# Key lists in three parts: attention over 64 queries where only one half of a query tile needs the keys

## The chip, the core and the metric

The kernel runs on one NeuronCore of a Trainium2 chip. The metric is the device time of one execution in microseconds. The kernel before takes 2263.21 us (median of three executions, 2261.73 to 2263.39). The profile shown below is of one execution with a span of 2257.2 us.

## What is computed

One layer of a graph transformer over 4096 nodes with 512 features, in float32. The adjacency matrix holds only zeros and ones and is sparse: node i and node j are joined with a probability that falls with both indices, so early nodes have many neighbours and late ones few.

```python
def gnn(node_matrix, adjacency, Wks, Wqs, Wvs, Wo):        # 8 heads of 64
    adj = maximum(adjacency, eye)
    q, k, v = node_matrix @ (Wqs, Wks, Wvs)                # per head
    scores = q @ k.T * 64 ** -0.5 + 0.01 * eye - 1e16 * (1 - adj)
    return einsum('hqm,hmk,hko->qo', softmax(scores), v, Wo)

x = x + gnn(layernorm(x), adj, ...)
x = x + moe_ffn(layernorm(x))       # 8 experts, each token goes to its best 2
```

A masked score has weight zero in the softmax. So for a query only its neighbours and itself have to be looked at.

## The kernel before

The 4096 queries are cut into 32 tiles of 128. For each query tile the kernel makes a list of the keys that at least one of its 128 queries is joined to, gathers those keys' rows 128 at a time, and runs attention on the gathered tiles alone. `LISTED` holds how many list tiles each query tile gets (363 in all); one more tile per query tile is the diagonal one (c = -1), so there are 395 items of attention.

**Stage one** projects x to k, v and q, and builds the lists beside it. Per query tile, VectorE reduces the adjacency to a flag for each key, counts flags, and GpSimd compares slot numbers with the running count (`begun`). TensorE then turns the comparison into the rows of the list with one matmul for each list tile, and VectorE computes the key numbers. `pack` already gathers two fifths of the mask tiles while GpSimd is there, and stores them packed, so that SyncE can fetch them later with a plain transfer.

```python
def neighbours(i):                      # one flag per key: is it joined to any of the 128 queries
    nc.vector.tensor_reduce(flags[g][:, j, :], adj_in.pop(i), axis=AX.X, op=ALU.max)

def begun(i):
    n = listed[i] * P
    nc.gpsimd.tensor_scalar(
        started[i], slots[:, :n], base[g][:, j : j + 1], None, op0=ALU.is_ge)

def list_rows(i, k):
    ...
    for t in range(m):
        nc.tensor.matmul(pr[:, t, :], started[i][:, ts(t0 + t, P)], row_x[g][:, j, :], ...)

def pack():
    i, c = ready.pop(0)
    m = work.tile([P, P], F32, tag="mask", bufs=6)
    gather(m, adjT_rows, mask_of, i, c)
    nc.sync.dma_start(out=packed_d[packed[i, c]], in_=m)
...
        if u < 8 * NTB - 4:             # at the end of each of 60 steps of stage one
            for _ in range(min(3, len(ready))):
                pack()
```

**Attention** runs over the 395 items in order, software-pipelined. Gathers run nine items ahead into ten buffers. In one round of the loop TensorE turns the keys of item n+3, computes the scores of item n+2 and multiplies the values of item n; between them stand pieces of work on query tiles that are done (sums, output projection, gate).

```python
def fetch(n):
    gather(kv[n], kv_d, key_of, i, c)                     # 128 rows of 4 KB, by GpSimd
    if (i, c) in packed:
        nc.sync.dma_start(out=mask[n], in_=packed_d[packed[i, c]])
    else:
        gather(mask[n], adjT_rows, mask_of, i, c)         # 128 rows of 512 B, by GpSimd

def turn(n):            # 8 transposes of 64 x 128
    nc.tensor.transpose(pk[:, r, ts(p, KD)], kv[n][half, ts(p, P)], ident[half, half])
    ...                 # then ScalarE copies PSUM to kT[n]

def scores(n):          # for each of 8 heads: keys are the weights, queries the moving side
    nc.tensor.matmul(s[r][:, p, :], k[rows, p, :], q_in[i][rows, p, :], start=True, stop=True)
    ...
    nc.scalar.activation(e[:, r * NP : (r + 1) * NP], s[r], AF.Exp)

def masked(n):
    nc.vector.tensor_mul(e, e, m.unsqueeze(1).to_broadcast([P, 2 * NP, P]))

def values(n):          # for each of 8 heads: values are the weights, e the moving side
    nc.tensor.matmul(po[i][r * KD : (r + 1) * KD, p, :], v[:, ts(h, KD)], e[:, r * NP + p, :], ...)
    ...
    nc.vector.tensor_add(acc[i], acc[i], e)
```

The profile counts two LDWEIGHTS and two MATMULs for each float32 matmul, and one of each for a transpose. The heads come in pairs that lie in different rows (scores, turn) or columns (values) of the array.

**Stage three** runs the expert layers on the routed tokens. If a list was too short for its keys, a general path recomputes all; with these inputs it does not run.

Of the kernel before, what the change touches and what calls it, by code (L numbers as in the profile page):

```python
# [12 lines left out]
I32 = mybir.dt.int32  # L13
AF = mybir.ActivationFunctionType
# [13 lines left out]
    10, 10, 9, 9, 9, 9, 9, 9, 9, 8, 8, 8, 8, 8, 8, 8,  # L28
]
# [3 lines left out]
def kernel(  # L33
# [50 lines left out]
    listed = [min(n, NT) for n in LISTED]  # L84
    at = [sum(listed[:i]) for i in range(NT + 1)]
# [8 lines left out]
    adjT_rows = adjT.rearrange("i k q -> (i k) q")  # L94

# [15 lines left out]
    longer = const.tile([P, NT], F32, name="longer")  # L111
# [78 lines left out]
    packed_d = dram.tile([NT * max(listed), P, P], F32, name="packed_d")  # L190
    waiting = []
# [11 lines left out]

    def fetch(n):

        i, c = items[n]
        kv[n] = kvp.tile([P, KV], F32, tag="kv", name=f"kv_{i}_{c}")
        mask[n] = kvp.tile([P, P], F32, tag="mask", name=f"mask_{i}_{c}")
        if c < 0:
            nc.sync.dma_start(out=kv[n], in_=kv_d[ts(i, P), :])  # L210
            nc.sync.dma_start(out=mask[n], in_=adjT[i, ts(i, P), :])
            return
        gather(kv[n], kv_d, key_of, i, c)
        if (i, c) in packed:
            nc.sync.dma_start(out=mask[n], in_=packed_d[packed[i, c]])
        else:
            gather(mask[n], adjT_rows, mask_of, i, c)

        if waiting and n % 3 == 0:
            waiting.pop(0)[1]()  # L220
# [9 lines left out]
    with tc.tile_pool(name="wqkv", bufs=1) as wp, tc.tile_pool(name="p1", bufs=3) as work, tc.tile_pool(  # L230
# [18 lines left out]
        for n, src, queue in (("k", Wks, nc.scalar), ("v", Wvs, nc.scalar), ("q", Wqs, nc.sync)):  # L249
            for c in range(DC):  # L250
# [14 lines left out]
        )  # L265

# [10 lines left out]
        slots = lp.tile([P, max(listed) * P], F32, bufs=1, name="slots")  # L277
        nc.gpsimd.iota(slots, pattern=[[1, max(listed) * P]], base=0, channel_multiplier=0,
                       allow_small_or_imprecise_dtypes=True)
# [3 lines left out]
        room = lp.tile([P, NT], F32, bufs=1, name="room")  # L283
        for i in range(NT):
            nc.gpsimd.memset(room[:, i : i + 1], float(listed[i] * P))
        again_c = lp.tile([P, G, C], F32, bufs=1, name="again_c")
        zero = lp.tile([1, KV], F32, bufs=1, name="zero")

        def list_constants():
            nc.vector.tensor_sub(step, ident, step)  # L290
            nc.vector.tensor_mul(other, other, part)
            nc.vector.tensor_scalar(other, other, -1.0, 1.0, op0=ALU.mult, op1=ALU.add)
            nc.vector.memset(again_c, 1.0)
            nc.vector.memset(again_c[:, :, 0:1], 0.0)
            nc.vector.memset(zero, 0.0)
            nc.sync.dma_start(out=kv_d[N : N + 1, :], in_=zero)
# [7 lines left out]
        def neighbours(i):  # L304

            g, j = divmod(i, G)
            if j == 0:
                flags[g] = lp.tile([P, G, C], F32, tag="flags", name=f"flags_{g}")
            nc.vector.tensor_reduce(flags[g][:, j, :], adj_in.pop(i), axis=AX.X, op=ALU.max)  # L309

        def count_1(g):

            f = flags.pop(g)
            nc.vector.tensor_mul(
                f, f, other[:, ts(g, G)].unsqueeze(2).to_broadcast([P, G, C])
            )
            upto = lp.tile([P, G, C], F32, tag="upto", name=f"upto_{g}")
            nc.vector.tensor_tensor_scan(
                upto.rearrange("p j c -> p (j c)"), again_c.rearrange("p j c -> p (j c)"),
                f.rearrange("p j c -> p (j c)"), initial=0.0, op0=ALU.mult, op1=ALU.add,  # L320
            )
            x_g = lp.tile([P, G, NX], BF16, tag="x", name=f"x_{g}")
            nc.vector.tensor_copy(x_g[:, :, :C], upto)
            row_x[g] = x_g

        def count_2(g):
            x_g = row_x[g]
            pb = ps_a.tile([P, 2, G], F32, tag="a", name=f"pb_{g}")
            nc.tensor.matmul(pb[:, 0], below, x_g[:, :, C - 1], start=True, stop=True)
            nc.tensor.matmul(pb[:, 1], ones, x_g[:, :, C - 1], start=True, stop=True)  # L330
            base[g] = pb

        def count_3(g):
            x_g, pb = row_x[g], base[g]
            b = lp.tile([P, G], F32, tag="base", name=f"base_{g}")
            nc.vector.tensor_copy(b, pb[:, 0])
            nc.vector.tensor_tensor(longer[:, ts(g, G)], pb[:, 1], room[:, ts(g, G)], op=ALU.is_gt)  # L337

            most = lp.tile([P, G, NT], F32, tag="most", name=f"most_{g}")
            nc.vector.tensor_tensor(  # L340
                most, b.unsqueeze(2).to_broadcast([P, G, NT]),
                full.unsqueeze(1).to_broadcast([P, G, NT]), op=ALU.is_ge,
            )
            hi = lp.tile([P, G], F32, tag="hi", name=f"hi_{g}")
            nc.vector.tensor_reduce(hi, most, axis=AX.X, op=ALU.add)
            lo = lp.tile([P, G], F32, tag="lo", name=f"lo_{g}")
            nc.vector.scalar_tensor_tensor(lo, hi, -float(P), b, op0=ALU.mult, op1=ALU.add)
            nc.vector.tensor_copy(x_g[:, :, C], hi)
            nc.vector.tensor_scalar_add(x_g[:, :, C + 1], lo, float(P))
            nc.vector.tensor_copy(x_g[:, :, C + 2], number.to_broadcast([P, G]))  # L350
            base[g] = b

        def steps(g):

            pd = ps_a.tile([P, G, NX], F32, tag="a", name=f"pd_{g}")
            nc.tensor.matmul(pd, step, row_x[g], start=True, stop=True)
            x_g = lp.tile([P, G, NX], BF16, tag="dx", name=f"dx_{g}")
            nc.scalar.copy(x_g, pd)
            row_x[g] = x_g

        def begun(i):

            g, j = divmod(i, G)
            n = listed[i] * P
            started[i] = lp.tile([P, n], BF16, tag="started", name=f"started_{i}")
            nc.gpsimd.tensor_scalar(  # L366
                started[i], slots[:, :n], base[g][:, j : j + 1], None, op0=ALU.is_ge
            )
# [4 lines left out]
        def list_rows(i, k):  # L373

            g, j = divmod(i, G)
            t0, m = chunks(i)[k]
            pr = ps_l.tile([P, CHUNK, NX], F32, tag="l", name=f"pr_{i}_{t0}")
            for t in range(m):
                nc.tensor.matmul(
                    pr[:, t, :], started[i][:, ts(t0 + t, P)], row_x[g][:, j, :],  # L380
                    start=True, stop=True,
                )
            rows_of[i, k] = pr

        def list_keys(i, k):
# [20 lines left out]
            nc.vector.tensor_scalar_add(mask_of[:, to], key, float(i * (N + 1)))  # L406
# [99 lines left out]
        def pack():  # L506
            i, c = ready.pop(0)
            m = work.tile([P, P], F32, tag="mask", bufs=6, name=f"pm_{i}_{c}")
            gather(m, adjT_rows, mask_of, i, c)
            packed[i, c] = len(packed)  # L510
            nc.sync.dma_start(out=packed_d[packed[i, c]], in_=m)
# [222 lines left out]
    with tc.tile_pool(name="p2a", bufs=2) as two, tc.tile_pool(  # L734
# [56 lines left out]

        def scores(n):

            i, c = items[n]
            s = [ps_s.tile([P, NP, P], F32, tag="s", name=f"s{r}_{i}_{c}") for r in range(2)]
            k = kT.pop(n)
            for p in range(NP):
                for r in range(2):
                    rows = slice(r * KD, (r + 1) * KD)
                    nc.tensor.matmul(  # L800
                        s[r][:, p, :], k[rows, p, :], q_in[i][rows, p, :],
                        start=True, stop=True,
                    )
            if c < 0:
                e = two.tile([P, 2 * NP, P], F32, tag="acc", name=f"acc_{i}")
                acc[i] = e
            else:
                e = work.tile([P, 2 * NP, P], F32, tag="e", name=f"e_{i}_{c}")
            for r in range(2):
                nc.scalar.activation(e[:, r * NP : (r + 1) * NP], s[r], AF.Exp)  # L810
            es[n] = e

        def masked(n):
            e, m = es[n], mask.pop(n)
            if items[n][1] < 0:
                nc.vector.tensor_max(m, m, eye_d)
            nc.vector.tensor_mul(e, e, m.unsqueeze(1).to_broadcast([P, 2 * NP, P]))  # L817

        def values(n):
# [4 lines left out]
            v = kv.pop(n)[:, H * KD :]  # L824
            for p in range(NP):
                for r in range(2):
# [3 lines left out]
                        po[i][r * KD : (r + 1) * KD, p, :], v[:, ts(h, KD)], e[:, r * NP + p, :],  # L830
# [3 lines left out]
            if c >= 0:  # L834
                nc.vector.tensor_add(acc[i], acc[i], e)  # L835
# [188 lines left out]
        bad = small.tile([P, NT, 3], F32, name="bad")  # L1024
        nc.vector.tensor_single_scalar(bad[:, :, 0], fine[:, :, 0], HIGH, op=ALU.is_lt)
        nc.vector.tensor_single_scalar(bad[:, :, 1], fine[:, :, 1], 1.0 / LOW, op=ALU.is_lt)
        nc.vector.tensor_single_scalar(bad[:, :, 2], longer, 0.5, op=ALU.is_lt)
# [264 lines left out]
```

## Time and profile before

| stage of the trace | us from the span's start | length, us | TensorE busy, us | VectorE busy, us | GpSimd busy, us |
|---|---|---|---|---|---|
| projections and lists (after the start) | 60 to 440 | 380 | 324.8 | 290.6 | 254.5 |
| seam | 440 to 468 | 28 | 20.7 | 5.4 | 13.2 |
| attention | 468 to 1645 | 1177 | 1149.3 | 1040.7 | 860.4 |
| seam | 1645 to 1700 | 55 | 19.4 | 18.2 | 7.8 |
| experts | 1700 to 2257 | 557 | 546.0 | 166.9 | 110.6 |

Busy times are of the instructions themselves; about 0.3 us after each gather in which GpSimd can't start the next is not in them. In the profile, L800 is the scores' matmul, L829 that of the values, L784 the turning of keys; L810 is the exponential, L787 ScalarE's copy of the turned keys; L817 and L835 are VectorE's mask product and sum; L199 is any gather, L366 the comparison of `begun`, L590 the last small matmul of the gate. PE is TensorE, PEld its weight loads, DVE VectorE, ACT ScalarE, POOL GpSimd.

### The profile page before, as it was taken

Reading aid. Unit: us, or ns where it says so; the run is one execution under the profiler, and the core shown is the slowest. Engines: PE = TensorE matmul, PEld = TensorE weight load, DVE = VectorE, ACT = ScalarE, POOL = GpSimd, SP = SyncE. Lnnn points to the kernel's source line nnn. Section 1 sums busy time; section 2 is a strip of 40 time slices with the busy share of each in tenths; the row PEclk is TensorE's granted clock in tenths of the full one; section 3 lists DMA queues with packets and bytes.
Section 4 is the critical chain, followed back from the end, with each engine's and each line's share of the span. In section 5 each row is a group of like instructions: output and inputs, shape, how many; then the busy total and the mean of one; then the engine's idle time right before and its main releaser. Section 6 shows DMA issues by size and latency. Waiting matters only on the chain. (4 is left out here: it accounts for less than half of the span.)

```text
span 2257.2 us, 51565 instructions
## 1 busy us (share of the span) xinstructions
PE 2104.6 (93%) x20304; PEld 1404.5 (62%) x20304; DVE 1550.2 (69%) x2300; ACT 966.7 (43%) x1834; POOL 1252.9 (56%) x943
## 2 busy tenths in 40 slices
PE   7788887989999999999999999999839999999998
PEld 3344443478888788787777887777724444444443
DVE  4888778279999888898888889888842332323332
ACT  2222221256666556566565565656412222222221
POOL 1467766668887687677686767778511121121121
PEclk9999998999999999999999999999969999999999
DMA  7768989577787788778787877767576566556654
GB/s 287 288 228 298 316 302 314 171 235 245 249 266 244 218 259 264 222 245 262 211 277 235 259 230 227 252 197 231 170 253 137 131 140 140 132 140 137 135 135 89
DMA packets 215031, 494.85 MB, mean 219 GB/s; under 512 B 27345, under 2 KB 81873, under 8 KB 210690
## 3 DMA queue, kind: packets, MB, share of 16 engines
q0 software_dynamic: 79232, 249.68, 37.6%
q1 hardware_dynamic: 134402, 239.71, 33.7%
q8 instruction: 165, 2.70, 0.5%
q10 hardware_dynamic: 1152, 2.10, 0.3%
q14 instruction: 80, 0.66, 0.1%
HBM read 410.95 MB, written 80.44 MB: 218 GB/s over the span
## 5 line engine op out<-in xcount | busy, mean ns | idle before, releaser
L199 POOL DMA_INDIRECT kv<-kv_d,key_of x363 | 514.2, 1417 | 211.2 <-PE po L829 117.3
L817 DVE TENSOR_TENSOR e<-e,mask 128x1024 f32<-128x1024 f32 x363 | 444.0, 1224 | 88.2 <-ACT e L810 87.1
L835 DVE TENSOR_TENSOR acc<-acc,e 128x1024 f32<-128x1024 f32 x363 | 442.9, 1220 | 0.0
L810 ACT ACTIVATE e<-s 128x512 f32<-128x512 f32 x726 | 394.6, 596 | 98.4 <-PE s L800 94.5
L800 PE MATMUL s<-q,kT 64*128 64x128 f32 x5808 | 411.4, 281 | 5.1 <-ACT acc L810 5.1
L829 PE MATMUL po<-e,kv 128*64 128x128 f32 x5808 | 399.5, 280 | 0.0
L1227 POOL DMA_INDIRECT out_dram<-y,r x71 | 110.6, 1558 | 471.8 <-ACT y L1226 432.2
L800 PEld LDWEIGHTS s<-q,kT 64*128 64x128 f32 x5808 | 363.2, 191 | 5.4 <-ACT acc L810 5.4
L787 ACT COPY kT<-pk 128x512 f32<-128x512 f32 x395 | 232.0, 587 | 263.0 <-PE pk L784 258.3
L829 PEld LDWEIGHTS po<-e,kv 128*64 128x64 f32 x5808 | 311.6, 137 | 44.4 <-issue 1.0
L199 POOL DMA_INDIRECT mask<-in_adjT_dram,mask_of x230 | 283.5, 1233 | 70.1 <-issue 55.5
L1191 PE MATMUL ph<-w,xT 128*128 x568 | 257.8, 596 | 0.7 <-ACT xT L182 0.7
L1220 PE MATMUL py<-w,hT 128*128 x568 | 255.6, 593 | 0.9 <-DVE hT L1205 0.9
L1225 DVE TENSOR_TENSOR y<-py,bb 128x512 f32<-128x512 f32 x71 | 49.1, 692 | 225.6 <-PE py L1220 225.6
L784 PE MATMUL pk<-ident,kv 64*128 64x64 f32 x2904 | 169.6, 236 | 15.3 <-ACT kT L787 14.7
L309 DVE TENSOR_REDUCE flags<-adjT 128x32 f32<-128x4096 f32 x32 | 141.2, 4412 | 58.7 <-DMA adjT<-in_adjT_dram 58.6
L366 POOL TENSOR_SCALAR started<-slots,base 128x1152 bf16<-128x1152 f32 (+11 forms) x32 | 126.5, 3952 | 97.9 <-DVE longer L337 86.4
L784 PEld LDWEIGHTS pk<-ident,kv 64*128 64x128 f32 x2904 | 119.9, 139 | 91.9 <-issue 63.5
L199 POOL DMA_INDIRECT pm<-in_adjT_dram,mask_of x133 | 128.1, 963 | 79.0 <-DMA packed_d<-pm 47.5
L1191 PEld LDWEIGHTS ph<-w,xT 128*128 128x128 f32 x568 | 103.1, 192 | 103.7 <-issue 102.6
L1220 PEld LDWEIGHTS py<-w,hT 128*128 128x128 f32 x568 | 102.5, 190 | 104.0 <-issue 102.8
L1196 DVE TENSOR_TENSOR h<-ph,bb 128x512 f32<-128x512 f32 x71 | 49.1, 692 | 138.8 <-PE ph L1191 138.8
(577 smaller groups left out, 2338.3 us busy)
## 6 DMA issues: line engine op xcount, KB each, us to landing
adjT<-in_adjT_dram SPq DMA_DIRECT2D x32, 2048.0 KB
bb<-in_L_ffn_b_dram SPq DMA_DIRECT2D x142, 256.0 KB
r<-xs_d SPq DMA_DIRECT2D x71, 258.0 KB
kv_d<-kv SPq DMA_DIRECT2D x32, 512.0 KB
packed_d<-pm SPq DMA_DIRECT2D x133, 64.0 KB
mask<-packed_d SPq DMA_DIRECT2D x133, 64.0 KB
xt<-in_x_dram SPq DMA_DIRECT2D x32, 256.0 KB
qT_d<-qT SPq DMA_DIRECT2D x8, 1024.0 KB
```

The costliest lines, as they stand in the source:

```text
L199: nc.gpsimd.indirect_dma_start(out=to, out_offset=None, in_=src, in_offset=bass.IndirectOffsetOnAxis(ap=of[:, at[i] + c : at[i] + c + 1], ...
L309: nc.vector.tensor_reduce(flags[g][:, j, :], adj_in.pop(i), axis=AX.X, op=ALU.max)
L366: nc.gpsimd.tensor_scalar(started[i], slots[:, :n], base[g][:, j : j + 1], None, op0=ALU.is_ge)
L784: nc.tensor.transpose(pk[:, r, ts(p, KD)], kv[n][half, ts(p, P)], ident[half, half])
L787: nc.scalar.copy(kT[n].rearrange("k p (r j) -> k r p j", r=2), pk[:, :, : NP * KD].rearrange("k r (p j) -> k r p j", p=NP),)
L800: nc.tensor.matmul(s[r][:, p, :], k[rows, p, :], q_in[i][rows, p, :], start=True, stop=True,)
L810: nc.scalar.activation(e[:, r * NP : (r + 1) * NP], s[r], AF.Exp)
L817: nc.vector.tensor_mul(e, e, m.unsqueeze(1).to_broadcast([P, 2 * NP, P]))
L829: nc.tensor.matmul(po[i][r * KD : (r + 1) * KD, p, :], v[:, ts(h, KD)], e[:, r * NP + p, :], start=(c < 0 and p == 0), stop=(c == listed[i ...
L835: nc.vector.tensor_add(acc[i], acc[i], e)
L1191: nc.tensor.matmul(ph, xTs[b][:, c, :], w1[:, bass.ds(es[b], 1), c, :], start=(c == 0), stop=(c == DC - 1),)
L1220: nc.tensor.matmul(py, hTs[b][:, c, :], w2[:, bass.ds(es[b], 1), c, :], start=(c == 0), stop=(c == HC - 1),)
```

## The change

Each list is built in three parts: first keys that only the first 64 queries need, then keys that both halves need, then keys that only the last 64 need. Two new tables hold, for each query tile, up to which list tile only the first half is concerned (`FIRST_ALONE`, 100 tiles in all) and from which one only the second half is (`SECOND_FROM`, 129 tiles in all). So 229 of the 363 list tiles belong to one half, and 134 to both. On a tile of one half, scores, exponential, mask product, values and sum run for 64 queries instead of 128, and the mask gather fetches rows of 256 B instead of 512 B. The number of items, of gathers and of packed tiles stays what it was.

It is for dropping work on queries that can't see a tile's keys.

The cost is in the lists: flags per half, counts for three parts, and a comparison for each part. A list tile that all parts may reach into needs three comparisons and three matmuls instead of one. GpSimd's comparisons go from 32 over 46,464 slots to 96 over 80,768, and read int16 slot numbers instead of float32 ones; TensorE's list matmuls go from 363 to 631.

```diff
+FIRST_ALONE = [ 10, 6, 5, 5, 4, 4, 4, 4, 3, ... 2, 2, 2 ]
+SECOND_FROM = [ 25, 14, 12, 10, 10, 9, 8, 8, 8, ... 5, 5, 5 ]
+    halves = [(min(a, n), min(b, n)) for a, b, n in zip(FIRST_ALONE, SECOND_FROM, listed)]
+    def half_of(i, c):
+        if c < 0:
+            return None
+        a, b = halves[i]
+        return 0 if c < a else 1 if c >= b else None
+    adjT_halves = adjT.rearrange("i k (h q) -> (i k h) q", h=2)
 ...
+    def gather_mask(m, i, c):
+        if half_of(i, c) is None:
+            gather(m, adjT_rows, mask_of, i, c)
+        else:
+            gather(m[:, :QH], adjT_halves, mask_of, i, c)
 ...
-            nc.vector.tensor_reduce(flags[g][:, j, :], adj_in.pop(i), axis=AX.X, op=ALU.max)
+            nc.vector.tensor_reduce(
+                flags[g][:, :, j, :], adj_in.pop(i).rearrange("p c (h q) -> p h c q", h=2),
+                axis=AX.X, op=ALU.max,
+            )
 ...  (count_1, count_2, count_3, steps: the same on three parts instead of one)
-        slots = lp.tile([P, max(listed) * P], F32, bufs=1, name="slots")
+        slots = lp.tile([P, max(listed) * P], I16, bufs=1, name="slots")
 ...
+        def ranges(i):
+            a, b = halves[i]
+            return [(0, b), (a, b), (a, listed[i])]
         def begun(i):
-            n = listed[i] * P
-            nc.gpsimd.tensor_scalar(
-                started[i], slots[:, :n], base[g][:, j : j + 1], None, op0=ALU.is_ge
-            )
+            for k, (t0, t1) in enumerate(ranges(i)):
+                nc.gpsimd.tensor_scalar(
+                    started[i, k], slots[:, t0 * P : t1 * P], base[g][:, k, j : j + 1], None,
+                    op0=ALU.is_ge,
+                )
 ...
             for t in range(m):
-                nc.tensor.matmul(pr[:, t, :], started[i][:, ts(t0 + t, P)], row_x[g][:, j, :], ...)
+                of = [(0, 0)] if h == 0 else [(2, 3)] if h == 1 else [(0, 0), (1, 1), (2, 2)]
+                for n, (q, r) in enumerate(of):
+                    nc.tensor.matmul(pr[:, t, :], started[i, q][:, s], row_x[g][:, r, j, :], ...)
 ...
+        def part(t, i, c):              # the first heads * 64 columns of a tile, as [P, heads, 64]
 ...
-                        s[r][:, p, :], k[rows, p, :], q_in[i][rows, p, :],
+                        part(s[r], i, c)[:, p, :], k[rows, p, :], q_in[i][rows, p, q],
-                nc.scalar.activation(e[:, r * NP : (r + 1) * NP], s[r], AF.Exp)
+                nc.scalar.activation(e[:, r * NP : (r + 1) * NP], part(s[r], i, c), AF.Exp)
-            nc.vector.tensor_mul(e, e, m.unsqueeze(1).to_broadcast([P, 2 * NP, P]))
+            m = mask_part(m, i, c)
+            nc.vector.tensor_mul(e, e, m.unsqueeze(1).to_broadcast(e.shape))
-                        po[i][r * KD : (r + 1) * KD, p, :], v[:, ts(h, KD)], e[:, r * NP + p, :],
+                        po[i][r * KD : (r + 1) * KD, p, q], v[:, ts(h, KD)], e[:, r * NP + p, :],
-                nc.vector.tensor_add(acc[i], acc[i], e)
+                nc.vector.tensor_add(acc[i][:, :, q], acc[i][:, :, q], e)
```

## The prediction

> **What bounds the kernel now.** I began with the busy times by stage, because the change touches only two stages. The columns are the stretch, its length, busy us of PE, PEld, DVE, ACT and POOL with instruction counts, the granted clock, the share of the DMA engines, and GB/s.
>
> ```profile
> 60.00:440.00 380.00, 324.83 (x1140) 151.28 (x1139) 290.58 (x489) 80.27 (x140) 254.53 (x165) 0.92 0.80 275
> 468.00:1645.00 1177.00, 1149.31 (x17193) 941.05 (x17192) 1040.74 (x1253) 728.09 (x1434) 860.42 (x635) 0.99 0.75 236
> 1700.00:2257.00 557.00, 546.04 (x1688) 268.89 (x1688) 166.94 (x350) 130.40 (x212) 110.60 (x71) 1.00 0.59 131
> ```
>
> Attention is 1177 us, with TensorE busy 98% of it, VectorE 88%. GpSimd shows 73%, but its roughly 635 gathers and scatters each have 0.3 us after them, so it is nearer 89%. The experts don't change. A busy TensorE is not yet TensorE at its limit, so I opened the timeline on a clean stretch (start, duration, engine, line).
>
> ```profile
> 483.77 0.46 PE L784 MATMUL pk<-ident,kv 64*128 64x64 f32 x8
> 483.97 1.28 DVE L817 TENSOR_TENSOR e<-e,mask 128x1024 f32<-128x1024 f32 x1
> 484.07 1.11 PE L800 MATMUL s<-q,kT 64*128 64x128 f32 x16
> 485.11 1.09 PE L829 MATMUL po<-e,kv 128*64 128x128 f32 x16
> 485.18 1.21 DVE L835 TENSOR_TENSOR acc<-acc,e 128x1024 f32<-128x1024 f32 x1
> 486.14 0.46 PE L784 MATMUL pk<-ident,kv 64*128 64x64 f32 x8
> 486.33 1.23 DVE L817 TENSOR_TENSOR e<-e,mask 128x1024 f32<-128x1024 f32 x1
> ```
>
> One item takes 486.14 - 483.77 = 2.37 us on TensorE, back to back: 0.24 to turn the keys (the scores' weight loads start at 484.01), 1.10 for scores, 1.03 for values. VectorE's two operations fill the same 2.36. TensorE sets the pace: 395 items x 2.37 = 936 us, and the other 241 of 1177 are the pieces between items (output projection, sums, gate). In the list of waits TensorE waits for a gathered tile for 0.6 us in all; GpSimd waits 117 us for TensorE to free a buffer. So gathers are ahead now.
>
> What halving the columns is worth depends on whether weights or moving columns set the pace. A row of the same trace separates them:
>
> ```profile
> 1596.91 0.30 PEld L590 LDWEIGHTS pl<-gather,l 128*128 128x128 f32 x2 [0.17 <-issue]
> 1596.91 0.39 PE L590 MATMUL pl<-gather,l 128*128 128x8 f32 x2
> ```
>
> Two loads of 128 float32 columns, 189 ns each by the tile's own view, cover 0.30 us, so they start 0.11 us apart, although only 8 columns move. 0.11 us is also the scores' step: 8 pairs of instructions in 0.89 us. The turning of keys, with 64 moving columns and pairs in different rows of the array, takes 0.24 us for 4 pairs, 0.06 us a pair.
>
> For the lists I looked at GpSimd's comparisons by shape:
>
> ```profile
> L366 POOL TENSOR_SCALAR started<-slots,base 128x1024 bf16<-128x1024 f32 x7 | 20.0, 2855 | 0.2
> L366 POOL TENSOR_SCALAR started<-slots,base 128x3584 bf16<-128x3584 f32 x1 | 9.3, 9346 | 60.0 <-DVE longer L337 60.0
> ```
>
> 2560 more slots cost 6.49 us: 2.54 ns a slot and 0.26 us an instruction.
>
> **What the skill says.** The Trainium skill, "TensorE: Matmul & The Clock Gate", LDWEIGHTS (loading the stationary operand), has a load cost by its columns, about P / 1.2 ns, and not by its rows: 107 ns for 128 columns. The 0.11 us above agrees; for the 64 columns of the values an estimate from that page is 53 ns. The same page, Packing small matmuls, has loads and matmuls in different rows or columns of the array run together; the scores' pairs at 0.11 us agree for rows. "SBUF — State Buffer", Who interferes with whom, says that a VectorE instruction with two SBUF inputs blocks a GpSimd instruction that reads SBUF. In attention, gathers take 0.94 us or up to 1.9, mean 1.42 for keys; in stage one, with few such products, mask gathers have a mean of 0.96. That fits. "GPSIMD Engine Reference", Elementwise — side-by-side cycle accounting, calls about 1.8 cycles per element at 1.2 GHz a good case; the 2.54 ns here are 3.0, and the trace counts. No page gives int16 against float32 on GpSimd.
>
> **The change, part by part.**
>
> *Scores of a half tile.* The weights stay 64 x 128 for each head, so the 0.11 us step stays. Only the last pair's stream is shorter: 1.10 becomes 1.05.
>
> *Values of a half tile.* The weights have 64 columns. With 64 moving columns I take the 0.06 us a pair of the turning. Now 1.03 = 8 x 0.11 + 0.15; then 8 x 0.06 + 0.15 = 0.63.
>
> *Sum.* 0.24 + 1.05 + 0.63 = 1.92 us against 2.37: 0.45 us x 229 half tiles = 103 us, all on the path if TensorE stays the bound. Not half of 229 x 2.13 us, because scores hardly gain.
>
> *VectorE, beside it.* Products and sums go from 1.22 us to about 0.69 (a 128x512 product elsewhere takes 0.68, row L871): 229 x 2 x 0.53 = 243 us less work. It was no bound, so I count only 5 us for rounds in which both engines now wait on each other.
>
> *ScalarE, beside it.* 512 columns take 587 ns, 128 take 265 (row L585): 0.84 ns a column, so 256 take 0.37. A half item costs 0.59 + 2 x 0.37 = 1.33 us, below 1.92.
>
> *GpSimd in attention.* The gathers stay: about 355 + 225, and 56 scatters. At today's means they need 355 x 1.72 + 225 x 1.53 + 56 x 1.66 = 1048 us, 0.3 us each included, against 1177 - 103 = 1074. If VectorE's blocks halve, the gathers get shorter, about 1.2 us by estimate: 580 x 1.5 + 93 = 963 us, 90% of the stage. That is tight for lists whose tiles are mostly halves; I add 12 us of waits.
>
> *Lists.* GpSimd: 80,768 x 2.54 ns + 96 x 0.26 = 230 us, now 126.5: +103. Of it 25 fall on the first four lists, where GpSimd still idles; +78 fall between 127 and 440 us, where its idle time, gap by gap in the timeline, is 52 us. It becomes the busiest engine there. TensorE reads a comparison one to two steps of some 7 us after it is asked for, so a lag of a few us is free. TensorE and VectorE wait some 50 us there already, partly for the 2 MB loads of the adjacency, and part of the lag hides in that. VectorE's counts over three parts add about 2.4 us to each of 8 groups, TensorE's 268 more list matmuls 0.03 us each, 8 us. I take +20 us for the stage, from 0 to +45.
>
> *DMA.* Half masks move 229 x 32 KB = 7 MB less in attention; at a share of 0.75 that buys nothing.
>
> Sum: 2263 - 103 - 5 + 12 + 20 = 2187; I say 2188.
>
> **Rivals.** (1) *Moving columns set the scores' step too:* then a half item is 1.92 - 8 x 0.05 = 1.5 us, 195 us saved by TensorE; but GpSimd's 963 would stand against 982, and the time would stop near 2130. Against it: the 8-column matmul at 0.11 us. (2) *The values' loads do not run together:* 2 x 53 ns a pair is the present 0.11, only the drains shrink, 0.10 x 229 = 23 us, and the kernel lands at 2255 to 2265. For it: no row before has 64 columns both loaded and moving in column pairs. Against: the loads of the values come in pairs a few ns apart. (3) *GpSimd becomes the bound in attention:* if gathers stay at 1.42 and 1.23 us, 1048 of 1074 leaves no slack, 15 to 30 us of waits, 2200 to 2215. (4) *The lists cost more:* if int16 slots are slower on GpSimd, or TensorE's in-order waits on comparisons add up, stage one grows by 60 or more: 2230.
>
> **Range and chances.** The saving of 103 has about 20 us to either side if the step of 0.06 holds, the lists 20, GpSimd 12; together about 32, so 2145 to 2240 should hold it 8 times in 10, with the longer tail up for rivals 2 to 4. 2% faster is below 2218: 0.78. Within 2%: 0.18. Slower by over 2%, above 2308, needs rival 2 and 4 together and more: 0.04.
>
> **What would show it.** In the profile after: half scores still start their pairs 0.11 us apart, half values 0.06 apart; items of 1.92 us; the attention stage near 1081 us with TensorE busy 97%; mask products of 0.69 us; gathers with a mean near 1.2 us; comparisons of 2.5 ns a slot, 230 us in all; stage one ending near 460 instead of 440. The prediction is wrong if values keep 0.11 us (rival 2), if TensorE waits for gathers by more than 30 us, or if comparisons hold up the list matmuls by more than 45 us.

## The result, and the profile after

The changed kernel takes **2204.76 us** (median of four executions, 2195.4 to 2206.74) against 2263.3: a ratio of 0.9733, with a 95% interval of 0.9704 to 0.9762. The prediction was 2188 us, in a range of 2145 to 2240. The profiled execution has a span of 2203.7 us, 53.5 less than before. The trace places that difference:

| Part of the span, us | before | after | difference |
|---|---|---|---|
| start to the end of the last list matmul | 440.2 | 482.6 | +42.4 |
| from there to the first turning of keys | 14.5 | 14.5 | 0 |
| attention, first turning of keys to the start of the last values | 1186.5 | 1093.0 | -93.5 |
| the rest (experts) | 615.9 | 613.6 | -2.4 |

So attention gave what was expected of it, and the lists cost twice what was expected. First the busy times by stage of the changed kernel (stretch, length, busy us of PE, PEld, DVE, ACT and POOL with counts, granted TensorE clock, DMA share, GB/s):

```profile
60.00:440.00 380.00, 309.18 (x1297) 147.68 (x1297) 289.57 (x524) 74.02 (x131) 318.09 (x197) 0.89 0.72 247
440.00:500.00 60.00, 56.40 (x219) 26.38 (x218) 14.68 (x60) 13.58 (x24) 48.05 (x41) 0.98 0.45 130
500.00:1600.00 1100.00, 1073.51 (x17275) 897.12 (x17273) 807.57 (x1296) 632.92 (x1444) 751.83 (x645) 0.96 0.79 252
```

In the first line GpSimd has risen from 254.5 to 318.1 us of 380, and it is now busier than TensorE. In the last, TensorE still sets the pace of attention (98% busy), and VectorE has fallen to 73%. The granted clock is 0.96, where before it was 0.99; that small figure turns out to matter.

The timeline of the same trace, TensorE alone (start, duration, engine, line), shows two half items back to back:

```profile
871.91 1.06 PE L922 MATMUL s<-q,kT 64*128 64x64 f32 x16
872.89 0.69 PE L954 MATMUL po<-e,kv 128*64 128x64 f32 x16
873.51 0.46 PE L893 MATMUL pk<-ident,kv 64*128 64x64 f32 x8
873.81 1.06 PE L922 MATMUL s<-q,kT 64*128 64x64 f32 x16
874.79 0.69 PE L954 MATMUL po<-e,kv 128*64 128x64 f32 x16
875.41 0.46 PE L893 MATMUL pk<-ident,kv_-1_9318 64*128 64x64 f32 x8
```

From 873.51 to 875.41 an item takes 1.90 us. The prediction's terms were 0.24 for the turning, 1.05 for scores and 0.63 for values, together 1.92. The groups by shape show the other engines (busy us, mean ns, then idle time before them):

```profile
L941 DVE TENSOR_TENSOR e<-e,mask 128x512 f32<-128x512 f32 x229 | 158.0, 690 | 143.3 <-ACT e L932 142.3 <-DMA mask<-in_adjT_dram,mask_of 0.3
L932 ACT ACTIVATE e<-s 128x256 f32<-128x256 f32 x458 | 151.5, 383 | 60.6 <-PE s L922 58.6 <-issue 1.8
L225 POOL DMA_INDIRECT kv<-kv_d,key_of x363 | 430.4, 1186 | 231.8 <-PE po L954 136.4 <-issue 32.3 <-PE pp L739 14.3
L457 POOL TENSOR_SCALAR started<-slots,base 128x896 bf16<-128x896 int16 x17 | 42.8, 2519 | 0.1
L457 POOL TENSOR_SCALAR started<-slots,base 128x384 bf16<-128x384 int16 x17 | 21.1, 1240 | 0.0
```

A half mask product takes 690 ns and an exponential of 256 columns 383. Key gathers have shrunk from 1417 to 1186 ns although they move the same rows. That VectorE's shorter products beside them are the cause is what the prediction argued; no run took this apart from the rest of the narrower work. GpSimd still waits for TensorE to free a buffer (136.4 us, 117.3 before), and not the other way round. The last two lines give the comparisons' price: 512 more slots cost 1279 ns, 2.50 ns a slot, with int16 slots as before with float32.

Where the lists lose their time is in the list of waits of stage one, 60 to 500 us (total, times, longest):

```profile
POOL started L457 <- DVE longer L407: 75.7, 2, 60.1
PEld L476 <- POOL started L457: 40.7, 23, 4.6
PE pr L476 <- POOL started L457: 31.9, 20, 3.2
PE pb L383 <- DVE x L377: 19.0, 5, 7.0
```

The second and third lines are one and the same wait of TensorE, seen at its weight loads and at its matmuls: 23 times, up to 4.6 us, 41 us in all. The fourth line has not moved (19.0 us before too). The first is the wait of the earliest comparisons for the counts, 75.7 us with one of 60; before it was 86.4 with one of 60. The load's wait in the trace before, where the list matmul is L379:

```profile
PEld L379 <- POOL started L366: 7.6, 3, 6.4
```

The 0.04 of clock that attention lost can be looked at in one stretch near its start and one later (same columns as the windows above):

```profile
508.00:532.00 24.00, 24.00 (x278) 22.14 (x276) 9.53 (x15) 8.34 (x22) 10.90 (x12) 0.50 0.71 221
700.00:724.00 24.00, 24.00 (x472) 21.68 (x472) 19.05 (x25) 15.75 (x36) 19.12 (x17) 1.00 0.84 268
```

Both show TensorE busy for 24.00 of 24 us; in the first it did 278 matmuls and in the second 472. A busy share can't tell them apart, only the clock column and the counts. In the first stretch the timeline has half items of 3.37 us instead of 1.90. By the clock records, TensorE was at half clock for 85.3 us of attention after, and 37.5 before.

### The profile page after: what moved, and what is told of

The parts are those of the page before. It is cut to its first block, busy times and chain, and to the rows that moved or that the text cites. A ratio compares the mean times of both kernels' runs of the same rounds, so it can differ in the third digit from the quotient of the medians.

```text
span 2203.7 us, 52479 instructions
## 1 busy us (share of the span) xinstructions
PE 2040.5 (93%) x20620; PEld 1366.7 (62%) x20620; DVE 1319.2 (60%) x2387; ACT 870.1 (39%) x1842; POOL 1242.8 (56%) x1072
## 5 line engine op out<-in xcount | busy, mean ns | idle before, releaser
L225 POOL DMA_INDIRECT kv<-kv_d,key_of x363 | 430.4, 1186 | 231.8 <-PE po L954 136.4
L941 DVE TENSOR_TENSOR e<-e,mask 128x512 f32<-128x512 f32 (+1 forms) x363 | 322.6, 889 | 204.0 <-ACT e L932 200.4
L922 PE MATMUL s<-q,kT 64*128 64x64 f32 (+1 forms) x5808 | 409.4, 282 | 2.7 <-ACT acc L932 2.7
L932 ACT ACTIVATE e<-s 128x256 f32<-128x256 f32 (+1 forms) x726 | 297.1, 461 | 101.5 <-PE s L922 98.6
L960 DVE TENSOR_TENSOR acc<-acc,e 128x512 f32<-128x512 f32 (+1 forms) x363 | 320.4, 883 | 1.4 <-PE po L954 1.4
L954 PE MATMUL po<-e,kv 128*64 128x64 f32 (+1 forms) x5808 | 311.3, 251 | 0.0
L457 POOL TENSOR_SCALAR started<-slots,base 128x384 bf16<-128x384 int16 (+12 forms) x96 | 229.0, 2401 | 76.6 <-DVE longer L407 75.7
L954 PEld LDWEIGHTS po<-e,kv 128*64 128x64 f32 x5808 | 246.4, 141 | 34.7 <-issue 0.8
L352 DVE TENSOR_REDUCE flags<-adjT 128x64 f32<-128x4096 f32 x32 | 141.2, 4413 | 81.2 <-DMA adjT<-in_adjT_dram 81.2
L1353 ACT ACTIVATE y<-y,gate 128x512 f32<-128x512 f32 x71 | 51.2, 722 | 213.1 <-DVE y L1352 213.1
```

The lines of the kernel that those rows point to most:

```text
L225: nc.gpsimd.indirect_dma_start(out=to, out_offset=None, in_=src, in_offset=bass.IndirectOffsetOnAxis(ap=of[:, at[i] + c : at[i] + c + 1], ...
L352: nc.vector.tensor_reduce(flags[g][:, :, j, :], adj_in.pop(i).rearrange("p c (h q) -> p h c q", h=2), axis=AX.X, op=ALU.max,)
L457: nc.gpsimd.tensor_scalar(started[i, k], slots[:, t0 * P : t1 * P], base[g][:, k, j : j + 1], None, op0=ALU.is_ge,)
L922: nc.tensor.matmul(part(s[r], i, c)[:, p, :], k[rows, p, :], q_in[i][rows, p, q], start=True, stop=True,)
L932: nc.scalar.activation(e[:, r * NP : (r + 1) * NP], part(s[r], i, c), AF.Exp)
L941: nc.vector.tensor_mul(e, e, m.unsqueeze(1).to_broadcast(e.shape))
```

## The experiments

**The traces so far are of one chip, here called A. All experiments ran on four others, B to E, on which the kernel before takes 2399 to 2413 us instead of 2263;** each figure below is therefore given against runs of the kernel before on its own chip. Where an expectation speaks of the first group it means chip B, and the last group is the one on C. Lines are those of the changed kernel unless said.

### Attention whole, lists in three parts

The helper that tells a list tile's half answers "both" for attention and packing, while the lists are still built in three parts. All list tiles run for 128 queries.

```diff
+    def half_a(i, c):
+        return None
-        if half_of(i, c) is None:          # in the mask fetches, queries() and part()
+        if half_a(i, c) is None:
```

> Lists in three parts as in the change, attention over all 128 queries of every tile as before the change (masks of 512 B). The theory that the time is a sum of two separate parts, lists +43 us and attention -93 us, gives 2263 + 43 = 2306 us, the attention stage at about 1186 us again and the end of the list matmuls at 482 us. If the longer stage one came from half-width transfers or from anything in attention's start, it would be shorter, near 2263 to 2280.

Chip B: 2444.08 us, ratio 1.0174 (1.0140 to 1.0208): 45 us slower than before. The last list matmul ends at 481.2 us. On chip B, then, the lists by themselves cost about what the traces of A put on them, 42.4 us. Attention over whole tiles gives none of it back.

### Comparisons of the lists on VectorE

```diff
-                nc.gpsimd.tensor_scalar(
+                nc.vector.tensor_scalar(
                     started[i, k], slots[:, t0 * P : t1 * P], base[g][:, k, j : j + 1], None,
```

> The changed kernel with the 96 slot comparisons moved from GpSimd to VectorE, nothing else. Theory G (GpSimd's 229 us of comparisons beside 133 gathers hold up TensorE's list matmuls): TensorE's wait for comparisons, 32 us now, is gone, the last list matmul comes at 440 to 452 us instead of 482, and the kernel takes 2165 to 2180 us. Theory V (VectorE's three-part counts are what lengthens stage one): VectorE gets still more work, so stage one stays at 480 or grows, 2200 to 2225 us.

Chip B: 2353.17 us, ratio 0.9814 (0.9779 to 0.9848). The last list matmul ends at 422.4 us, sooner than the 440 to 452 expected. The same kernel again on chip C, with the changed kernel itself beside it:

> The 96 comparisons of the lists on VectorE instead of GpSimd, all else as in the change. In the first group they took 0.3 to 0.5 us there instead of 1.2 to 3.2, and attention began at 437 instead of 497 us. If the comparisons on GpSimd are what holds up the lists: attention begins 55 to 62 us sooner than in the changed kernel beside it, and the whole is 45 to 60 us faster than it. If the lists' stage is bound by something else on another chip: under 20 us.

Chip C: 2353.5 us against 2412.88 for the changed kernel beside it, 59 less. Attention starts at 439.4 instead of 498.6 us, so the whole gain is in the lists. The comparisons by shape (busy us, mean ns, idle before), and below them TensorE's wait for them in the list of waits of stage one, 60 to 500 us:

```profile
L457 DVE TENSOR_SCALAR started<-slots,base 128x896 bf16<-128x896 int16 x17 | 7.9, 465 | 0.0
L457 DVE TENSOR_SCALAR started<-slots,base 128x384 bf16<-128x384 int16 x17 | 5.7, 336 | 0.0
```
```profile
PEld L476 <- DVE started L457: 1.7, 2, 1.5
```

512 slots more cost 129 ns here against 1279 on GpSimd; all 96 comparisons take 37.5 us instead of 229. The wait of 41 us is 1.7. VectorE, 76% busy in that stretch already, absorbed them. It was not the number of list matmuls, nor the flags and counts for three parts, that held up the lists.

The control for this is the kernel before with its 32 comparisons moved in the same way:

> The kernel before, lists in one part, with only its 32 comparisons moved from GpSimd to VectorE: what the move is worth without the change. In the kernel before, the list matmuls waited for GpSimd's comparisons only 10.6 us in all, and VectorE's waits on other things stay. If the move helps mainly what the change had added: 0 to 20 us faster than the kernel before beside it, so that some 60 us of the gain of the best version belong to the change of the attention together with the move. If GpSimd was already what set the end of the lists in the kernel before: 30 us or more.

Chip E: 2384.98 us, ratio 0.9923 (0.9899 to 0.9948), 15 us faster. Its last list matmul ends at 420.6 us; with the change and the same move it ends at 424.9 on chip C, and between 422.4 and 428.0 in the five traces with that move. Off GpSimd, the three-part lists thus cost 2 to 7 us, not 42.

### The changed kernel once more

> The changed kernel itself once more, on the chip of this group, so that the variants beside it can be read against it. If the 59 us that it gained do not depend on the chip: 2.5 to 3% below the kernel before of the same group. If the chip is one on which TensorE often stands still inside an item for waits that the profile does not name (as it did in the first group, where the kernel before took 2399 us and attention with 128 queries 1329 us), theory: those pauses come with the items and not with their width, so the gain stays 50 to 60 us; rival: the granted half clock, met more often when items are narrow and there are pauses, eats a part of it, and the gain is only 0 to 25 us (the first group's version with another order of the same items gained 1 us).

> The changed kernel itself, for the variants beside it. Two kinds of chip have been met. If this group falls on one like the first (kernel before 2263 us): 55 to 65 us faster than the kernel before, with 85 us of half clock in the attention stage. If on one like the two groups since (kernel before about 2400 us, TensorE standing still for short pauses inside items): within 15 us of the kernel before, with some 250 us of half clock in the attention stage.

Chip C: 2412.88 us against 2403.95 before (ratio 1.0034, 1.0006 to 1.0061). Chip D: 2425.24 against 2412.78 (1.0050, 1.0031 to 1.0068). **On these chips the change makes the kernel slightly slower.** The loss lies outside what the expectations for chip C named. The lists cost the same, and attention gains less: 1289.2 and 1310.5 us, where the kernel before with moved comparisons (chip E), whose attention is that of the kernel before, has 1321.5. Attention is at half clock for 266 and 290 us, against 109 in that control. The timeline of TensorE on chip C shows how such a spell begins (start, duration, engine, line, and in brackets the idle time before):

```profile
648.66 0.46 PE L893 MATMUL pk<-ident,kv 64*128 64x64 f32 x8
648.96 1.79 PE L922 MATMUL s<-q,kT 64*128 64x64 f32 x16
650.67 0.70 PE L954 MATMUL po<-e,kv 128*64 128x64 f32 x5
651.75 0.40 PE L954 MATMUL po<-e,kv 128*64 128x64 f32 x6 [0.38 <-issue]
653.22 0.48 PE L954 MATMUL po<-e,kv 128*64 128x64 f32 x4 [1.07 <-issue]
654.63 0.26 PE L954 MATMUL po<-e,kv 128*64 128x64 f32 x1 [0.93 <-issue]
654.83 0.69 PE L893 MATMUL pk<-ident,kv 64*128 64x64 f32 x8
655.31 1.92 PE L922 MATMUL s<-q,kT 64*128 64x64 f32 x16
657.16 1.12 PE L954 MATMUL po<-e,kv 128*64 128x64 f32 x16
```

In the middle of one item's values TensorE stops three times, waiting for nothing the profile names ("issue"). At 652.4 the granted clock falls to half, and for 13.7 us an item takes 3.38 us (654.83 to 658.21). Such stops can be added up as steps of 0.4 us or more between two weight loads, leaving out the output projection, whose matmuls of 512 columns take 0.43 us each anyway and make some 109 us of such steps in every trace. They come to 46 us of attention before and 44 after on chip A; on the others to 162 and 169 us with whole tiles and 176 to 197 with half tiles. What makes TensorE stop there stays open: the stops follow no fetch, buffer or engine that I could find, and they are in the kernel before with moved comparisons as well (162 us). The experiments also came later than the first traces, so chip and time are not told apart.

### Order of the items

```diff
-    items = [(i, c) for i in range(NT) for c in range(-1, listed[i])]
+    def turn_of(i):                      # own tile, tiles of both halves, first, second
+        a, b = halves[i]
+        return [-1] + list(range(a, b)) + list(range(a)) + list(range(b, listed[i]))
+    items = [(i, c) for i in range(NT) for c in turn_of(i)]
```

> The changed kernel with another order of the items of a query tile in attention: the diagonal tile, the tiles of both halves, then those of the first and of the second half. The amount of work is the same. Theory C (after a pause TensorE's clock falls to half, and tiles of one half keep the array too little busy to bring it back soon, 41 us at the start of attention): with full tiles first the half clock ends within 10 to 15 us, and the kernel gains 8 to 15 us, 2190 to 2197. If the 41 us had nothing to do with the kind of tile, the time stays within 3 us of 2205.

Chip B: 2397.47 us, ratio 0.9998 (0.9975 to 1.0020), with 235.5 us of half clock in attention. That is 10 to 14 us better against before than the changed kernel was on C and D. On chip B itself the version with moved comparisons has the changed kernel's attention in the old order: 1287.8 us, 252.6 of them at half clock, against 1276.9 and 235.5 here. The first spell of attention lasts 17.1 us here and 44.4 there. So the order is worth about 11 us (one trace each), within the 8 to 15 expected, but most of the half clock comes in later spells and stays.

### Scores over 128 queries on every tile

The scores of a half tile run for all 128 queries and the exponential reads only the needed 64. Values, products and sums stay halved.

```diff
-                        part(s[r], i, c)[:, p, :], k[rows, p, :], q_in[i][rows, p, q],
+                        s[r][:, p, :], k[rows, p, :], q_in[i][rows, p, :],
-                nc.scalar.activation(e[:, r * NP : (r + 1) * NP], part(s[r], i, c), AF.Exp)
+                nc.scalar.activation(e[:, r * NP : (r + 1) * NP], s[r][:, :, q], AF.Exp)
```

> The changed kernel with the scores of every tile computed for all 128 queries; exponential, mask, values and sum stay at 64 on half tiles. Theory W (the weight loads set the scores' pace): the scores of a half tile go from 1.05 back to 1.10 us, 229 x 0.05 = 12 us more, 2217 us, or less if theory C holds and the fuller stream brings the clock back sooner: 2203 to 2212. If moving columns set the pace, 229 x 0.45 = 103 us more: above 2290.

> Scores over 128 queries on every list tile, values and the rest over 64 as in the change. By the medians of the trace a half item costs 0.053 us more, 12 us in 229 items, so this should be 12 us slower than the changed kernel beside it, if the width does not matter to the clock. Theory of the clock (narrow items keep TensorE from coming back to its full clock): the wider scores cut the time at half clock in the attention stage from 85 us to under 60, which gives back 0.45 of the difference, so the two come out within 8 us of each other or this one ahead.

Chip B: 2380.65 us, ratio 0.9919 (0.9894 to 0.9944). Chip C: 2388.92 us, ratio 0.9946 (0.9926 to 0.9966): TensorE is given more work, and the kernel is 24 us faster than the changed kernel beside it. Half clock in attention falls from 266.2 to 95.6 us; on chip B it is 78.5, against 252.6 in the version with moved comparisons. The windows of the two on chip C show it, the changed kernel first:

```profile
500.00:1700.00 1200.00, 1119.62 (x16078) 927.62 (x16079) 741.76 (x1143) 586.54 (x1336) 689.24 (x603) 0.89 0.71 217
```
```profile
500.00:1700.00 1200.00, 1112.45 (x16540) 902.71 (x16538) 760.88 (x1171) 601.13 (x1374) 696.36 (x621) 0.96 0.72 222
```

In the same 1200 us the second has 462 more matmuls with less busy time, and the clock column is the reason: 0.96 instead of 0.89. The stops hardly differ (188 and 179 us in attention).

### A dose in between, and the best version

The comparisons on VectorE together with the wide scores, twice, and once with scores over 96 queries:

```diff
+            wide = {None: slice(0, P), 0: slice(0, 96), 1: slice(32, P)}[half_of(i, c)]
-                        s[r][:, p, :], k[rows, p, :], q_in[i][rows, p, :],
+                        s[r][:, p, wide], k[rows, p, :], q_in[i][rows, p, wide],
```

> Both of the two above in one: comparisons on VectorE, and scores over 128 queries on every tile. If the two effects add and the clock theory holds: 45 to 65 us faster than the changed kernel beside it and the fastest of the four. If the wider scores only cost their 12 us: 35 to 48 us faster than it, and slower than the version with the comparisons alone moved.

> The version with the comparisons on VectorE and the scores over 128 queries once more. On a chip like that of the first traces: the lists end 55 to 60 us sooner than in the changed kernel, half clock in the attention stage falls from 85 to under 55 us, and the whole lies 50 to 70 us below the changed kernel beside it. On one like the last group's: 75 to 95 us below it, with about 95 us of half clock in the attention stage.

> As the version with the comparisons on VectorE and the scores over 128 queries, but on tiles of one half the scores run for 96 queries, the 64 that are needed and 32 beside them. If it is the number of moving columns that keeps TensorE at its full clock through pauses: the time at half clock lies between that of 64 columns (280 us with the comparisons moved, on the last group's chip) and that of 128 (96 us), nearer to neither, 140 to 220 us, and the whole 15 to 45 us above the version with 128 and below the version with 64. If it is that the wider item is 0.053 us longer (1.099 instead of 1.046 us at the medians), and so gives the other engines more time: an item of 96 is as long as one of 64 or 128, and the half clock goes with that length and not with the columns.

The best version takes 2327.35 us on chip C, ratio 0.9680 (0.9648 to 0.9712), and 2341.42 on D, 0.9707 (0.9636 to 0.9778). It is 85.5 and 84 us below the changed kernel beside it. That is the sum of the two single effects, 59.4 + 24.0 = 83.4; my first expectation of 45 to 65 was too low because it gave the scores nothing. With 96 columns it is 2344.92 us (0.9713, 0.9645 to 0.9781).

| chip D, columns of a half tile's scores | 64 (changed kernel) | 96 | 128 |
|---|---|---|---|
| half clock in attention, us | 290.1 | 157.0 | 109.2 |
| attention, us | 1310.5 | 1283.9 | 1272.5 |
| scores of a half item at full clock, us | 1.046 | 1.07 | 1.10 |
| stops of 0.4 us or more in attention, us | 197 | 191 | 187 |

The windows of the three, in the table's order:

```profile
500.00:1700.00 1200.00, 1114.32 (x15846) 926.62 (x15846) 729.78 (x1115) 576.59 (x1315) 672.81 (x592) 0.89 0.68 214
```
```profile
500.00:1700.00 1200.00, 1110.29 (x16213) 905.73 (x16211) 755.30 (x1180) 589.58 (x1354) 684.69 (x608) 0.94 0.70 217
```
```profile
500.00:1700.00 1200.00, 1113.04 (x16367) 898.19 (x16366) 762.63 (x1189) 594.97 (x1370) 695.52 (x608) 0.96 0.70 217
```

Half clock lies between, as the columns would have it. The item's length lies between too, so the table can't separate length and columns in themselves; a count further down does. The rival, that a longer item means fewer stops, explains little: the stops fall by 10 us, where attention falls by 38. The 15 to 45 us that I expected between 96 and 128 came out as 3.5 in the times (11 in attention), which is within their spread. The 64 column differs also in where the comparisons run; the version with 64 columns and moved comparisons had 279.9 us of half clock on chip C.

Not all of the best version's gain is the change's. The kernel before gains 0.8% by the move of the comparisons alone (ratio 0.9923 on chip E). Against that, the change with moved comparisons is 1.1 to 1.4% faster, and with the wide scores 2.2 to 2.5%; these ratios compare chips, each read against its own runs of the kernel before.

## Why the prediction was right, and where it was not

**TensorE's terms held.** The medians give a half item 0.409 us less in values and 0.053 in scores, 105.8 us in 229 items against the 103 of the sum. Weight loads set the scores' step, and the loads of a half item's values ran together, in pairs every 0.058 us, so rivals 1 and 2 are out. VectorE, ScalarE and GpSimd have the durations worked out for them: 0.690 us predicted as 0.69, 0.383 as 0.37, key gathers 1.186 as about 1.2, comparisons 229 us as 230.

**The 12 us of waits for gathers were a wrong term.** TensorE waited 0.4 us for a gather in all of attention, and rival 3 with it is out. In its place stands what the prediction does not mention, the granted clock. Of each microsecond at half clock, 1 - 1.90/3.37 = 0.44 is lost, so 85.3 instead of 37.5 us cost 21 us. Medians and half clock together give -85; of the 9 us to the measured -93.5 the prediction had named 5, the waits between VectorE and TensorE, and no run took those apart. That the stage came out right, -93.5 against -96, is therefore partly luck: one loss was put for another.

**The lists' +20 was mis-sized: it measured +42.4,** near the upper end of the 0 to 45 given. The failing step is "a lag of a few us is free", with its sequel that part of the lag hides in waits that are there already. The amount of comparisons was right; but once GpSimd is the busiest engine of the stage, its lag doesn't come once, it returns at list after list: 23 waits of TensorE, 41 us, where 7.6 had been; the prediction had set 45 as its sign of being wrong. That is the second half of rival 4, in-order waits that add up. The move to VectorE shows it by taking the wait and the time away together.

**What was right for one chip is not right for the next.** Chip B has both kinds of attention, whole tiles in the version with the lists alone, then half tiles in the one with moved comparisons:

```profile
495.70:1824.40 1328.70, 1233.88 (x17243) 992.56 (x17245) 1039.32 (x1262) 728.08 (x1438) 850.20 (x645) 0.96 0.67 213
436.90:1724.70 1287.80, 1202.28 (x17243) 993.94 (x17245) 803.02 (x1258) 629.27 (x1437) 725.11 (x641) 0.90 0.68 213
```

By the medians the second should be 105.8 us shorter. Half clock is 252.6 instead of 112.6 us, and 0.44 x 140 = 62 is taken back by that. This leaves 44, where 41 are measured. From E to C the same sum leaves 37, where 32 are measured (1321.5 to 1289.2); from E to D it leaves 26, and only 11 are measured, so it is good to some 15 us. With the lists' 42 the change then comes out at about nothing or a little slower, which is what chips C and D show.

The Trainium skill, "TensorE: Matmul & The Clock Gate", Part 1: The HAM clock gate, would have warned of it: it says that half clock is the default and that "activity releases the throttle", judged in windows of about 3.4 us. The traces agree on the window: the spells last 3.4, 6.8, 10.2, 13.7 or 17.1 us and so on, whole multiples of 3.41 except for the one that the end of a trace cuts off. What the page calls the abstract rule, "no PE-idle gaps >~3.4µs" (HAM oscillation — how this bites in real kernels), is not enough here: the stops above are each under 1.1 us, and the clock fell. Narrower tiles mean fewer columns moved per microsecond while the weight loads keep their pace, and I had priced the columns only by their time.

**What the clock goes by can be counted in the traces.** Cut at the changes of the clock, the stretch from 505 to 1580 us of all 14 traces gives 4409 windows of 3.41 us. For each, add up the moving columns of the matmuls that start in it (a matmul over 64 queries counts 64, and each of the two that the profile lists for a float32 matmul counts). After the 529 windows with at most 3008 columns the clock was half 467 times; after the 3880 with more, 41 times. That is 103 wrong, and leaving out any one trace gives the same limit. The best limit on TensorE's busy time gets 328 wrong, one on the longest pause 407, one on the number of matmuls 487. A half item at half clock, back to back, moves 2560 columns in 3.37 us, which is 2590 per window, so a stream of them does not bring the clock back; with scores over 128 queries it is 3584 in 3.49 us, 3510 per window, and with 96 it is 3072 in 3.43, 3050, just above the limit. So the clock goes with the columns moved in a window, and not with the length of one pause or of an item. The limit was fitted afterwards to these traces. Counting each column by the share of the array that its matmul fills does a little better (74 wrong), so columns and busy cells are not told apart.

## What to carry to other kernels

Where weight loads set the pace, dropping moving columns saves little (here 0.053 us of a half item's 1.10 us of scores) and can cost the clock: here 64 columns of scores that nobody reads bought 24 us. When work is added to an engine, compare its load with the stage and not with its idle time, and ask whether another engine does the same in a tenth of the time. Read the clock column with every busy share, and repeat a gain of 3% on another chip before believing it.

## What the runs showed of the hardware that was not expected

- A comparison of int16 slots against one value per partition, giving bf16, costs 2.50 ns a slot on GpSimd and 0.25 ns on VectorE (512 slots in 1279 and 129 ns).
- TensorE fell to half clock after pauses much shorter than the 3.41 us window, several of them in one window. In the changed kernel on chip C the longest step between two weight loads in the 3.41 us before a fall had a median of 1.05 us (23 falls between 510 and 1580 us), and the shortest was 0.58. These windows began 46 matmuls at most, where 72 of a half item fit (40 in 1.90 us).
- The same program took 2263 us on chip A and 2399 to 2413 on B to E, with nearly all of the difference in attention (1186 us on A against 1321 to 1329 in the two traces with whole tiles from other chips), while the part after attention took 614 to 616 us on A and 619 to 629 on the others.
